# Building convolution kernels from one shared angle, in groups of four and eight channels

## The chip, the cores and the metric

The kernel runs on one core of a Trainium2 chip. The engines are named as in the profile: PE (TensorE, the matrix multiplier, with PEld for its weight loads), DVE (VectorE), ACT (ScalarE), POOL (GpSimd) and SP (SyncE, which issues DMAs). The metric is device time in microseconds (us). Each time is the median of several runs; beside it stands one profiled execution, from which all durations of single instructions come.

## The reference

Four layers follow each other, each added to x (32 x 64 x 1024, float32). The first is a long convolution per channel, the next two multiply by one of 16 matrices that an index selects, the last is a gated feed-forward layer with low-rank additions. Only the first is touched:

```python
dt = exp(log_dt)                                  # per channel h
A  = -exp(log_A_real) + 1j * A_imag               # per channel and state, 64 states
Ct = C * (exp(A * dt) - 1) / A
K  = 2 * einsum('hn,hnl->hl', Ct, exp(A * dt * arange(L))).real
y  = causal_convolution(u, K) + u * D             # L = 1024
x  = x + y * (arange(L) < length)                 # a length for each of 32 batches
```

So 64 kernels K of 1024 taps have to be made from 64 complex states each, and every channel is then convolved with its kernel. D, a number per channel, can be added to tap 0 of K.

## The kernel before

`convolution` (line 598) holds this layer; `tile_cond_resid_kernel` (line 64) calls it and goes on with the adapters (line 161) and the feed-forward layer (line 456).

**Making K.** The 128 partitions hold the 64 states twice, the upper half for imaginary parts. Position l is written as 32 a + b, so that exp(A dt l) is a product of a coarse power (a) and a fine power (b), and K as a 32 x 32 matrix is a matmul of 128 partitions: coarse powers times coefficients (`gt`) against fine powers (`et`). Small tiles (`small`, 128 x 64) hold what exists per state and channel: the step, the exponents x and y, the coefficients. Sines go through `sine` (line 638): the angle is divided by 2 pi, rounded by adding and subtracting a large number (`MAGIC`), 2 pi times that is subtracted in three parts, a phase is added, the result is clamped to pi, and ACT takes the sine. A cosine is a sine with another phase, and its own reduction.

`kernels(g)` (line 738) makes the kernels of eight channels. POOL multiplies x and y by the 32 positions (`brho`, `bth`; lines 757, 758), ACT takes Exp of the one, DVE and ACT take three sines of the other (coarse cosine, coarse sine and one fine sine; lines 641 to 649), DVE forms `bgt` and `bet` with five products and sums (lines 777 to 781), PE multiplies (line 785, eight matmuls into `pk`), ACT copies `pk` to `ks` (line 793), POOL adds D to tap 0 (line 795), and ACT issues two stores to `kp` in HBM: 128 zeros per row, which are written early, and the row itself (line 798).

**Convolving.** `convolve` (line 803) handles four channels. SP loads `uf`, x with each block of 128 positions reversed (line 806), and `hk`: for each pair of channels a 128 x 1024 matrix with overlapping windows of the stored row (line 811), three buffers. PE multiplies, eight matmuls a channel with 256, 224, ... 32 columns (line 823); DVE multiplies the result by the mask into `tmp` (line 830), and POOL adds it into the four tiles of x (line 839), which SP loaded first of all (line 622).

**Order.** PE's order is the program's own. On DVE, ACT, POOL and SP a scheduler places the instructions, from the program and a model of their times; each engine then executes strictly in that order, and waits at an instruction whose inputs or buffers aren't free. Tiles of pool `s1` have one buffer, those of `s2` two. The loop at line 842 calls `kernels` for group 0, then after the first and the second four channels, and then after each group of eight, so that PE makes a group's rows one to two groups ahead of their use. SP also issues the adapters' first weight tiles (`early`, nine of them, and then `wa`, nine buffers; line 177) where the scheduler puts them among the `hk` loads.

Of the kernel before, what the change touches and what calls it, by code (L numbers as in the profile page):

```python
# [8 lines left out]
F32 = mybir.dt.float32  # L9
I32 = mybir.dt.int32  # L10
AF = mybir.ActivationFunctionType
ALU = mybir.AluOpType
# [23 lines left out]
NE = 16  # L36
NPIECE = 2 * BC
AT_GATED, AT_DOWN = 4, 5
HG = 8
LQ = 32  # L40
KROW = P + L

# [8 lines left out]


CO_LVAL = 0
CO_PHI = CO_LVAL + 2 * LQ
CO_SGN = CO_PHI + 4
CO_POS = CO_SGN + 1
CO_R = CO_POS + KT
CO_OFF = CO_R + 1
# [539 lines left out]
def convolution(tc, cst, consts, xt, xf, ssm, lens, xs, ps_tile):  # L598
# [9 lines left out]
    with ExitStack() as ctx:  # L608
# [25 lines left out]
        def tt(o, a, b, op):  # L634
            nc.vector.tensor_tensor(o, a, b, op)
            return o

        def sine(theta, phi, turns, new):

            k, r = new("k"), new("r")  # L640
            nc.vector.tensor_scalar(k, theta, 1.0 / TWO_PI, turns, ALU.mult, ALU.add)
            nc.vector.tensor_scalar(k, k, MAGIC, MAGIC, ALU.add, ALU.subtract)
            nc.vector.scalar_tensor_tensor(r, k, -C1, theta, ALU.mult, ALU.add)
            nc.vector.scalar_tensor_tensor(r, k, -C2, r, ALU.mult, ALU.add)
            nc.vector.scalar_tensor_tensor(r, k, -C3, r, ALU.mult, ALU.add)
            nc.vector.tensor_scalar(r, r, phi, PI_IN, ALU.add, ALU.min)
            nc.vector.tensor_scalar(r, r, -PI_IN, None, ALU.max)
            s = new("s")
            nc.scalar.activation(s, r, AF.Sin)
            return s  # L650

        def exponential(v):

# [21 lines left out]
            )  # L675
            return k


        x, y = small(), small()
        ex = exponential(par[:, 0:2, :].rearrange("p i h -> p (i h)"))  # L680
        dt, ea = ex[:, :H], ex[:, H:]
        nc.vector.scalar_tensor_tensor(x, ea, -1.0, dt, ALU.mult, ALU.mult)
        tt(y, aim, dt, ALU.mult)

        t, em, ep = small(), small(), small()
        nc.scalar.activation(t, x, AF.Tanh, scale=0.5)
# [4 lines left out]

        yh = small()
        nc.vector.tensor_scalar(yh, y, 0.5, None, ALU.mult)
        sh = sine(yh, 0.0, 0.0, lambda _: small())
        ch = sine(yh, math.pi / 2, 0.25, lambda _: small())
        zr, zi, u = small(), small(), small()
        nc.vector.scalar_tensor_tensor(u, ep, 2.0, sh, ALU.mult, ALU.mult)
        tt(zi, u, ch, ALU.mult)
        tt(u, u, sh, ALU.mult)
# [7 lines left out]
        tt(v, zi, cre, ALU.mult)  # L707
        tt(ni, ni, v, ALU.add)

        den, w, ctr, cti = small(), small(), small(), small()  # L710
        tt(den, ea, ea, ALU.mult)
        tt(w, aim, aim, ALU.mult)
        tt(den, den, w, ALU.add)
        nc.vector.reciprocal(den, den)
        nc.vector.tensor_scalar(den, den, col(CO_SGN), None, ALU.mult)
        tt(ctr, ni, aim, ALU.mult)
        tt(w, nr, ea, ALU.mult)
        tt(ctr, ctr, w, ALU.subtract)
        tt(ctr, ctr, den, ALU.mult)
        tt(cti, ni, ea, ALU.mult)  # L720
        tt(w, nr, aim, ALU.mult)
        nc.vector.scalar_tensor_tensor(cti, cti, -1.0, w, ALU.mult, ALU.subtract)
        tt(cti, cti, den, ALU.mult)


        lnf = s1.tile([P, B], F32, tag="lnf", name="lnf")
        nc.vector.tensor_copy(lnf, ln)
        mask = s1.tile([P, KT, B], F32, tag="mask", name="mask")
        for kt in range(KT):
            nc.vector.tensor_scalar(  # L730
                mask[:, kt, :], lnf, col(CO_POS + kt), None, ALU.is_gt
            )
        maskf = mask.rearrange("p k b -> p (k b)")

        zero = s1.tile([HG, P], F32, tag="zero", name="zero")
        nc.vector.memset(zero, 0.0)

        def kernels(g):

            h0 = g * HG  # L740
            shape = [P, HG, LQ]

            def over_l(ap):
                return ap[:, h0 : h0 + HG].unsqueeze(2).to_broadcast(shape)

            def over_h(at):
                return cst[:, at : at + LQ].unsqueeze(1).to_broadcast(shape)

            n = [0]

            def big(tag, pool=s1):
                n[0] += 1
                return pool.tile(shape, F32, tag=f"b{tag}", name=f"b{tag}{g}_{n[0]}")

            def powers(at, tag):
                theta, rho = big(f"th{tag}"), big(f"rho{tag}")
                nc.gpsimd.tensor_tensor(theta, over_l(y), over_h(at), ALU.mult)
                nc.gpsimd.tensor_tensor(rho, over_l(x), over_h(at), ALU.mult)
                nc.scalar.activation(rho, rho, AF.Exp)
                return theta, rho  # L760

            th1, rho1 = powers(CO_LVAL, "1")
            th2, rho2 = powers(CO_LVAL + LQ, "2")

            def flat_sine(theta, i, tag):
                return sine(
                    theta.rearrange("p h l -> p (h l)"),
                    col(CO_PHI + i),
                    col(CO_PHI + 2 + i),
                    lambda q: big(q if q == "k" else f"{q}{tag}").rearrange("p h l -> p (h l)"),  # L770
                ).rearrange("p (h l) -> p h l", l=LQ)

            p1 = flat_sine(th1, 0, "p")
            q1 = flat_sine(th1, 1, "q")
            p2 = flat_sine(th2, 0, "e")
            gt, et = big("gt", s2), big("et", s2)
            tt(et, p2, rho2, ALU.mult)
            tt(p1, p1, over_l(ctr), ALU.mult)
            tt(q1, q1, over_l(cti), ALU.mult)
            tt(p1, p1, q1, ALU.add)  # L780
            tt(gt, p1, rho1, ALU.mult)

            ps = ps_tile(f"pk{g}")
            for i in range(HG):
                nc.tensor.matmul(
                    ps[:LQ, i * LQ : (i + 1) * LQ],
                    gt[:, i, :],
                    et[:, i, :],
                    start=True,
                    stop=True,  # L790
                )
            ks = s2.tile([LQ, HG, LQ], F32, tag="ks", name=f"ks{g}")
            nc.scalar.copy(ks.rearrange("a h b -> a (h b)"), ps[:LQ, : HG * LQ])
            k0 = ks[0:1, :, 0]
            nc.gpsimd.tensor_tensor(k0, k0, dskip[0:1, h0 : h0 + HG], ALU.add)
            kp = dram.tile([HG, KROW], F32, tag=f"kp{g}", name=f"kp{g}")
            nc.scalar.dma_start(kp[:, :P], zero)
            nc.scalar.dma_start(kp[:, P:].rearrange("h (a b) -> a h b", b=LQ), ks)
            return kp

        loads = []
# [1 line left out]
        def convolve(kp, row, ha):  # L803

            uf = s3.tile([P, 4, KT, B], F32, tag="uf", name=f"uf{ha}", bufs=2)
            nc.sync.dma_start(uf, xf[:, ha : ha + 4])
            tmp = s2.tile([P, 4, KT * B], F32, tag="tmp", name=f"tmp{ha}")
            for i in range(0, 4, 2):
                hk = s3.tile([P, 2, L], F32, tag="hk", name=f"hk{ha + i}")

                load = nc.sync.dma_start(
                    hk,
                    bass.AP(
                        tensor=kp.tensor,
                        offset=kp[row + i : row + i + 1, 1:2].offset,
                        ap=[[1, P], [KROW, 2], [1, L]],
                    ),
                )
                loads.append(load.ins)
                ps = ps_tile(f"pc{ha + i}").rearrange("p (i t) -> p i t", i=2)  # L820
                for j in range(2):
                    for d in range(KT):
                        nc.tensor.matmul(  # L823
                            ps[:, j, d * B :],
                            hk[:, j, d * P : (d + 1) * P],
                            uf[:, i + j, : KT - d, :].rearrange("p k b -> p (k b)"),
                            start=(d == 0),
                            stop=(d == KT - 1),
                        )
                tt(  # L830
                    tmp[:, i : i + 2, :],
                    ps,
                    maskf.unsqueeze(1).to_broadcast([P, 2, KT * B]),
                    ALU.mult,
                )
            tv = tmp.rearrange("p i (k b) -> p k b i", b=B)
            for c in range(NCK):
                xv = xs[c].rearrange("p k (b h) -> p k b h", h=H)[:, :, :, ha : ha + 4]
                nc.gpsimd.tensor_tensor(xv, xv, tv[:, :, c * BC : (c + 1) * BC, :], ALU.add)


        ready = [kernels(0)]
        for ha in range(0, H, 4):
            convolve(ready[ha // HG], ha % HG, ha)

            if len(ready) < H // HG and (ha == 0 or ha % HG == 4):
                ready.append(kernels(len(ready)))
        return loads


# [1 line left out]
def _constants(np):  # L852
# [2 lines left out]
    c = np.zeros((P, CO_N), np.float32)  # L855
    c[:, CO_LVAL : CO_LVAL + LQ] = LQ * np.arange(LQ)
    c[:, CO_LVAL + LQ : CO_LVAL + 2 * LQ] = np.arange(LQ)
    for i, turns in enumerate((np.where(im, 0.0, 0.25), np.where(im, 0.25, 0.5))):
        c[:, CO_PHI + i] = TWO_PI * turns
        c[:, CO_PHI + 2 + i] = turns  # L860
    c[:, CO_SGN] = np.where(im, -2.0, 2.0)
    c[:, CO_POS : CO_POS + KT] = p[:, None] + P * np.arange(KT)
    c[:, CO_R] = p % R
# [137 lines left out]
```

## Time and profile before

| what | us |
|---|---|
| median of 3 runs (2413.58 to 2415.15) | 2414.2 |
| the profiled execution, its own time | 2413.82 |
| its span, first to last instruction | 2412.2 |
| PE busy in the span | 2322.5 |
| DVE, ACT, POOL busy | 1115.7, 306.7, 209.9 |
| first convolution matmul starts | 41.7 |
| first adapter matmul starts | 207.4 |

The page shows busy time per engine, then 40 slices of the span, DMA queues, the chain of work that ended last, and the costliest groups. Busy PE means that matmuls are in flight, not that it is at its peak. A timeline row gives start, duration, engine, line, tiles and count, with the idle time ahead of it and what ended that. A matmul of float32 leaves two records.

### The profile page before, as it was taken

How to read it: one execution, taken by the hardware profiler on the slowest of the kernel's cores; microseconds unless marked ns; L12 is line 12 of the kernel's file. 1: busy time of each engine (PE TensorE's matmuls, PEld its weight loads, DVE VectorE, ACT ScalarE, POOL GpSimd, SP SyncE). 2: the span in 40 equal slices, each digit the busy share in tenths (PEclk: the TensorE clock that was granted, in tenths of full speed). 3: DMA queues.
4: the chain of work that ended last, by engine and by line, in shares of the span. 5: the costliest groups of instructions: out<-in, count | busy, mean ns of one | idle time of the engine just before them, and what ended most of it. 6: DMA issues, size and time to landing. Idle time of an engine off the chain costs nothing.

```text
span 2412.2 us, 46245 instructions
## 1 busy us (share of the span) xinstructions
PE 2322.5 (96%) x19136; PEld 1834.6 (76%) x19136; DVE 1115.7 (46%) x2192; ACT 306.7 (13%) x597; POOL 209.9 (9%) x294
## 2 busy tenths in 40 slices
PE   3898888999999999999999999999999999999999
PEld 3896335777887786877787786787787787888888
DVE  8911113544354453454344543454344534655653
ACT  3200001111011101110011101110011101110110
POOL 2534001000000011000000020000000020000000
PEclk9999999999999999999999999999999999999999
DMA  6789997665665656665656646656756543223311
GB/s 242 247 289 347 408 408 286 245 231 199 229 214 208 225 158 202 231 219 201 219 210 222 235 141 218 225 203 211 242 192 244 201 147 119 88 79 112 98 56 62
DMA packets 163092, 501.20 MB, mean 208 GB/s; under 512 B 19970, under 2 KB 54082, under 8 KB 161858
## 3 DMA queue, kind: packets, MB, share of 16 engines
q1 hardware_dynamic: 146402, 461.76, 54.6%
q0 software_dynamic: 9568, 27.80, 3.5%
q10 hardware_dynamic: 6912, 8.69, 1.0%
q8 instruction: 151, 2.47, 0.4%
q14 instruction: 59, 0.48, 0.1%
HBM read 485.30 MB, written 12.88 MB: 207 GB/s over the span
## 4 chain that ended last, share of the span: by engine, by line
PE 88%; DMA 9%; DVE 2%; SPq 0%; issue 0%; ACT 0%; POOL 0%; DVEq 0%; ACTq 0%
PE pf L359 40%; PE po L556 20%; PE pa L182 14%; DMA wa<-in_w 7%; PE pc L823 5%; PE pr L419 3%; PE po L551 2%; PE pe L303 2%; PE pl_d L275 1%; DMA hk<-kp 1%; DMA wl<-in_wd_rest 1%; DMA early<-in_w 0%; PE pl_u L275 0%; PE pl_g L275 0%; DMA ln<-in_lens 0%
## 5 line engine op out<-in xcount | busy, mean ns | idle before, releaser
L359 PE MATMUL pf<-xd,wf 128*128 128x256 f32 x2560 | 607.2, 381 | 0.0
L359 PEld LDWEIGHTS pf<-xd,wf 128*128 128x128 f32 x2560 | 481.6, 190 | 75.4 <-issue 7.4
L182 PE MATMUL pa<-wa,x 128*32 128x256 f32 x8048 | 469.2, 382 | 30.6 <-DMA wa<-in_w 29.3
L359 PE MATMUL pf<-xd,s 128*128 128x256 f32 x1920 | 453.6, 379 | 0.4 <-ACT c L375 0.4
L182 PEld LDWEIGHTS pa<-wa,x 128*32 128x32 f32 x8048 | 246.2, 110 | 246.2 <-DMA wa<-in_w 71.8
L359 PEld LDWEIGHTS pf<-xd,s 128*128 128x128 f32 x1920 | 364.7, 190 | 50.4 <-ACT c L375 0.8
L823 PE MATMUL pc<-uf,hk 128*128 128x256 f32 (+7 forms) x1024 | 153.5, 313 | 17.9 <-DMA hk<-kp 17.2
L823 PEld LDWEIGHTS pc<-uf,hk 128*128 128x128 f32 x1024 | 148.7, 196 | 22.3 <-DMA hk<-kp 9.7
L219 POOL DMA_INDIRECT bgu<-in_bgu,rows x44 | 46.3, 1053 | 1351.0 <-PE pe L303 1304.0
L556 PE MATMUL po<-act,wd 128*128 128x256 f32 x640 | 161.7, 383 | 0.0
L556 PE MATMUL po<-actd,wd 128*128 128x256 f32 x640 | 159.0, 379 | 0.0
L556 PE MATMUL po<-actd,s 128*128 128x256 f32 x640 | 159.0, 379 | 0.0
L384 DVE TENSOR_TENSOR c<-pf,u 128x256 f32<-128x256 f32 x80 | 33.9, 424 | 242.3 <-PE pf L359 242.3
L556 PEld LDWEIGHTS po<-act,wd 128*128 128x128 f32 x640 | 119.5, 190 | 22.9 <-issue 6.1
L556 PEld LDWEIGHTS po<-actd,s 128*128 128x128 f32 x640 | 121.6, 190 | 16.5
L556 PEld LDWEIGHTS po<-actd,wd 128*128 128x128 f32 x640 | 121.6, 190 | 16.5
L313 ACT COPY lt<-pe 128x512 f32<-128x512 f32 x160 | 82.1, 600 | 307.5 <-PE pe L303 216.1
L193 DVE STREAM_TRANSPOSE y<-pa 128x512 f32<-128x512 f32 x64 | 45.4, 710 | 145.0 <-PE pa L182 145.0
L388 DVE TENSOR_TENSOR c<-c,lt 128x1024 f32<-128x1024 f32 x80 | 97.9, 1224 | 6.7 <-DVE c L386 0.5
L331 DVE TENSOR_TENSOR s<-wf 128x512 f32<-128x512 f32 x80 | 54.6, 683 | 81.3 <-DMA wf<-in_wg 38.5
L331 DVE TENSOR_TENSOR s<-wd 128x384 f32<-128x384 f32 x64 | 31.1, 486 | 128.9 <-PE po L556 96.0
L419 PE MATMUL pr<-x,wr 128*128 128x512 f32 x192 | 84.2, 595 | 0.0
(173 smaller groups left out, 1845.0 us busy)
## 6 DMA issues: line engine op xcount, KB each, us to landing
wa<-in_w SPq DMA_DIRECT2D x503, 512.0 KB, 8.2
wf<-in_wg SPq DMA_DIRECT2D x80, 512.0 KB, 4.4
wf<-in_wu SPq DMA_DIRECT2D x80, 512.0 KB, 3.6
wd<-in_wd SPq DMA_DIRECT2D x96, 384.0 KB, 4.3
hk<-kp SPq DMA_DIRECT2D x32, 1024.0 KB, 8.1
x<-in_xt SPq DMA_DIRECT2D x4, 2048.0 KB, 10.7
uf<-in_xf SPq DMA_DIRECT2D x16, 512.0 KB, 4.4
wd<-in_wd SPq DMA_DIRECT2D x32, 256.0 KB, 3.9
```

The lines of the kernel that those rows point to most:

```text
L182: nc.tensor.matmul(acc[i * S : (i + 1) * S, s * 256 : (s + 1) * 256], xs[c][:, kt, lo + s * S : lo + (s + 1) * S], wt[:, i * 256 : (i + 1) ...
L193: nc.vector.transpose(y, acc)
L219: nc.gpsimd.indirect_dma_start(out=t, out_offset=None, in_=table, in_offset=bass.IndirectOffsetOnAxis(ap=at_, axis=0),)
L303: nc.tensor.matmul(ps[:, at_ * 2 * H : (at_ + 1) * 2 * H], bt[pair(j), g], tms[table][pair(j)], start=(g == 0), stop=True, skip_group_chec ...
L313: nc.scalar.copy(lt[:, :n, 2 * H * j : 2 * H * (j + 1)], ps[:, : n * 2 * H].rearrange("p (i t) -> p i t", i=n),)
L331: nc.vector.tensor_add(s1, a21, a22)
L359: nc.tensor.matmul(ps, ws[j][:, kt, :], xb[j][:, kt, :], start=start and kt == 0, stop=kt == KH - 1, skip_group_check=True,)
L388: nc.vector.tensor_add(cf, cf, lt[:, g].rearrange("p i t -> p (i t)"))
L419: nc.tensor.matmul(ps, wt[:, kt, :], xs[c][:, kt, :], start=(kt == 0), stop=(kt == KT - 1),)
L551: nc.tensor.matmul(pss[j], w, a, start=False, stop=False, skip_group_check=True)
L556: nc.tensor.matmul(pss[j], ws[j][:, i, :], ab[m - m0][j], start=(m == m0 and home[j] % 2 == 0), stop=(m == m1 - 1), skip_group_check=True,)
L823: nc.tensor.matmul(ps[:, j, d * B :], hk[:, j, d * P : (d + 1) * P], uf[:, i + j, : KT - d, :].rearrange("p k b -> p (k b)"), start=(d == ...
```

## The change

The coarse and the fine angle stand in one tile `r` (two times n x 32 columns) and are reduced together, without a phase (`reduced`). ACT takes the sine of the coarse angle, and gets cosines as the sine of pi/2 minus the magnitude (`cosine`), in place of a second reduction; of the fine angle, the lower 64 partitions take the cosine and the upper 64 the sine. The upper half's coefficients are written out with operands that differ by half (`ax`, `ay`). Groups are 4, 4, 8, 8, ... channels instead of 8; the Exp factors of the first two are made first, ahead of the small tiles' Tanh and Sin (`sizes`, with an ordering edge). D reaches tap 0 through a matmul: a tile `dk`, zero but for D in one column per channel, times a selecting matrix, into the same PSUM accumulation (POOL writes D into `dk`, which has one buffer). The masks are one DVE operation in place of eight, after group 1's last product, and POOL converts the lengths. The first four channels' `hk` are loaded one channel at a time. Two groups are made ahead of the first `convolve`, and group g + 2 after the first four channels of group g.

```diff
-HG = 8
+GROUPS = (4, 4, 8, 8, 8, 8, 8, 8, 8)
+HG = max(GROUPS)
...
+        def reduced(theta, k):
+            nc.vector.tensor_scalar(k, theta, 1.0 / TWO_PI, MAGIC, ALU.mult, ALU.add)
+            nc.vector.tensor_scalar(k, k, MAGIC, None, ALU.subtract)
+            for part in (C1, C2, C3):
+                nc.vector.scalar_tensor_tensor(theta, k, -part, theta, ALU.mult, ALU.add)
+            nc.vector.tensor_scalar(theta, theta, PI_IN, -PI_IN, ALU.min, ALU.max)
+            return theta
+
+        def cosine(o, r, k):
+            nc.scalar.activation(k, r, AF.Abs)
+            nc.scalar.activation(o, k, AF.Sin, scale=-1.0, bias=col(CO_HALF))
...
+        def powers(g, v, pool, tag):
+            o = big(g, tag, pool, True)
+            for i in range(2):
+                at_ = cst[:, CO_LVAL + i * LQ : CO_LVAL + (i + 1) * LQ]
+                at_ = at_.unsqueeze(1).to_broadcast([P, GROUPS[g], LQ])
+                nc.gpsimd.tensor_tensor(o[:, i], over_l(g, v), at_, ALU.mult)
+            return o
...
+        def sizes(g):
+            rho = powers(g, x, s2, "rho")
+            done = nc.scalar.activation(rho, rho, AF.Exp)
+            sized.append(done.ins)
+            return rho
...
         tt(y, aim, dt, ALU.mult)
+        rhos = {g: sizes(g) for g in range(2)}
...
-        sh = sine(yh, 0.0, 0.0, lambda _: small())
-        ch = sine(yh, math.pi / 2, 0.25, lambda _: small())
+        reduced(yh, u)
+        with tc.issue_after(sized[-1]):
+            nc.scalar.activation(sh, yh, AF.Sin)
+            cosine(ch, yh, zr)
...
+        nc.scalar.copy(ax[re], aim[re])
+        nc.scalar.mul(ax[im], ea[im], -1.0)
+        nc.scalar.copy(ay[re], ea[re])
+        nc.scalar.copy(ay[im], aim[im])
...
-        nc.vector.tensor_copy(lnf, ln)
-        for kt in range(KT):
-            nc.vector.tensor_scalar(
-                mask[:, kt, :], lnf, col(CO_POS + kt), None, ALU.is_gt
-            )
...
+        dk = s1.tile([P, HG, LQ], F32, tag="dk", name="dk")
+        nc.gpsimd.memset(dk, 0.0)
 
         def kernels(g):
-            th1, rho1 = powers(CO_LVAL, "1")
-            th2, rho2 = powers(CO_LVAL + LQ, "2")
-            p1 = flat_sine(th1, 0, "p")
-            q1 = flat_sine(th1, 1, "q")
-            p2 = flat_sine(th2, 0, "e")
+            h0, n = sum(GROUPS[:g]), GROUPS[g]
+            rho = rhos.pop(g) if g in rhos else sizes(g)
+            r = powers(g, y, s1, "r")
+            nc.gpsimd.tensor_copy(dk[0:1, :n, 0], dskip[0:1, h0 : h0 + n])
+            k, co = big(g, "k", s1, True), big(g, "co", s1, True)
+            reduced(r, k)
+            cosine(co, r, k)
+            si = big(g, "si", s1, False)
+            nc.scalar.activation(si, r[:, 0], AF.Sin)
+            nc.scalar.activation(co[im, 1], r[im, 1], AF.Sin)
...
+            ps = ps_tile(f"pk{g}")[:LQ, : n * LQ]
+            nc.tensor.matmul(
+                ps,
+                cst[:, CO_SEL : CO_SEL + LQ],
+                dk[:, :n].rearrange("p h l -> p (h l)"),
+                start=True, stop=False, skip_group_check=True,
+            )
...
-            k0 = ks[0:1, :, 0]
-            nc.gpsimd.tensor_tensor(k0, k0, dskip[0:1, h0 : h0 + HG], ALU.add)
...
+                for j in range(0, 2, 1 if ha == 0 else 2):
+                    n = 1 if ha == 0 else 2
+                    load = nc.sync.dma_start(hk[:, j : j + n], ...)
...
-        ready = [kernels(0)]
+        ready = [kernels(0), kernels(1)]
+        nc.gpsimd.tensor_copy(lnf, ln)
+        with tc.issue_after(made[1]):
+            nc.vector.tensor_tensor(
+                mask,
+                lnf.unsqueeze(1).to_broadcast([P, KT, B]),
+                cst[:, CO_POS : CO_POS + KT].unsqueeze(2).to_broadcast([P, KT, B]),
+                ALU.is_gt,
+            )
+        for g, n in enumerate(GROUPS):
+            h0 = sum(GROUPS[:g])
+            for i in range(0, n, 4):
+                convolve(ready[g], i, h0 + i)
+                if i == 0 and g + 2 < len(GROUPS):
+                    ready.append(kernels(g + 2))
```

## The prediction

> **What bounds the kernel now.** I read, in this order: the page's shares and slices, PE's timeline over the first 225 us, the chain of waits for 50 to 72 and 190 to 262 us, 2-us stretches with clock and DMA share, and the groups by form. The change touches the convolution alone, which PE leaves at 207.4 us of a span of 2412.2. PE's timeline (start, us, engine, line, tiles, [idle before <-releaser]):
>
> ```profile
> 31.10 1.06 PE L785 MATMUL pk<-bet,bgt 128*32 128x32 f32 x16 [31.10 <-DVE bet L635]
> 41.69 11.36 PE L823 MATMUL pc<-uf,hk 128*128 128x256 f32 x64 [9.53 <-DMA hk<-kp]
> 52.98 0.69 PE L785 MATMUL pk<-bet,bgt 128*32 128x32 f32 x16
> 53.60 9.38 PE L823 MATMUL pc<-uf,hk 128*128 128x256 f32 x64
> 62.92 0.69 PE L785 MATMUL pk<-bet,bgt 128*32 128x32 f32 x16
> 70.93 21.27 PE L823 MATMUL pc<-uf,hk 128*128 128x256 f32 x128 [7.32 <-DMA hk<-kp]
> ...
> 170.50 36.98 PE L823 MATMUL pc<-uf,hk 128*128 128x256 f32 x256
> 207.41 0.64 PE L182 MATMUL pa<-early,x 128*32 128x256 f32 x8
> ```
>
> PE starts at 41.69, convolves channels 0 to 7, stands 7.32 us for channel 8's `hk`, and then hardly stands again (0.3 us at 121.6, 0.7 at 132.2). Four channels take 9.38 us. So the end of the stage hangs on the moment when channel 8 starts. The chain of waits (start, us, what) says who was late:
>
> ```profile
> 57.40 0.60 DVE tmp L635
> 58.00 0.07 issue
> 58.07 4.57 POOL x L839 x4
> 62.64 0.23 POOL ks L795
> 62.89 1.54 DMA kp<-ks
> 64.45 6.35 DMA hk<-kp
> ```
>
> Kernel rows that ACT had copied at 57.5 waited in POOL's queue, behind four additions into x, for an addition of 0.23 us; ahead of that the chain is DVE's sine reductions. After the convolution the chain is one stream of weights, whose start hangs on SP's last `hk` issue (193.7, when PE frees a buffer), not on PE's work; from 373 us on it is PE:
>
> ```profile
> 249.59 10.11 DMA wa<-in_w
> ...
> 259.81 10.11 DMA wa<-in_w
> ```
>
> Eight tiles take 10.11 us, 1.26 each. What the convolution wins thus reaches the end of the kernel, as does each `early` tile loaded before that last issue. Two stretches set bounds (span, PE, PEld, DVE, ACT, POOL busy, clock, DMA share, GB/s): x is still landing until about 27 us, and after its wait PE runs at half clock:
>
> ```profile
> 24.00:26.00 2.00, 0.00 (x0) 0.00 (x0) 2.00 (x7) 1.10 (x1) 1.03 (x1) 1.00 0.92 381
> 26.00:28.00 2.00, 0.00 (x0) 0.00 (x0) 1.93 (x6) 0.69 (x2) 1.26 (x2) 1.00 0.63 250
> 72.00:74.00 2.00, 2.00 (x8) 1.93 (x7) 2.00 (x3) 0.00 (x0) 2.00 (x3) 0.50 1.01 408
> ```
>
> **What the Trainium skill says.** *VectorE: DVE Perf Modes*, "The perf-mode tier table": fp32 `tensor_scalar` between SBUF tiles runs at twice the rate of `tensor_tensor`. The trace agrees: 0.28 us against 0.42 for 256 elements, and 0.69 for 512 with two inputs; from 0.18, 0.22, 0.28 for 64, 128, 256 I estimate 0.42 for one input at 512. *GPSIMD Engine Reference*, "Specifications": SBUF interfaces are shared with VectorE. It agrees: DVE operations of 0.42 take about 1.05 while POOL adds into x at 72 us. *ScalarE: Activation LUTs*, "Table sets: the hidden batching unit": `abs` is filler in every set, so it needs no load of its own; no run here shows it yet, but loads take the 1283 ns of its section "What ACT_TABLE_LOAD costs". *TensorE: Matmul & The Clock Gate*, Part 1: after an idle window of about 3.4 us PE runs at half clock until warm. It agrees: four channels after the first wait took 11.36 instead of 9.38, eight after the second 21.27 instead of 18.7.
>
> **The change, part by part.**
>
> *Masks later.* DVE now stands from 5.1 to 8.08 for `lens` (6.24 us to land), as mask operations stand among the exponential's steps. Without them eight dependent steps of 0.33 (0.28 plus 0.05) end at 7.7 instead of 10.9; x is ready at 8.0. POOL now converts `lens` ahead of its first product, and ACT's ninth store of zeros waits for the same DMA semaphore ahead of the Tanh, so both start at about 8.5: of 3.2 us some 2.7 are won.
>
> *Groups 0 and 1.* POOL makes the x products of both groups and then group 0's y: six of 128 elements. From 0.24 us for 8 elements and 0.61 to 0.66 for 256 I take 0.45: 8.5 + 2.7 = 11.2. DVE finishes the half angle and reduces group 0's two angles in one go (two `tensor_scalar`, three two-input steps, one clamp on 256 elements: 3 x 0.28 + 3 x 0.42 + gaps = 2.4) from 12.3 to 14.7. ACT needs 0.42 + 0.31 + 0.42 + 0.31 for magnitude, sine, cosine and the imaginary half: 16.1. DVE then has 17 coefficient operations and five products, mixed with group 1's reduction, about 0.18 apart: 20.4, against 31.0 now. PE's rows: 21. ACT copies them behind group 1's first activations and stores behind its cosine: issue at about 21.9, landed 23.9.
>
> *`hk` by single channels.* Issued at 23.9, but SP's queue still holds x until about 27. Half a MB after that, with the 6.35 of the chain less 1.7: 29.7. PE starts there instead of at 41.69. The two extra issues cost 0.4 us each on SP, under x's tail; `uf` of channels 4 to 7, now behind these loads on SP, is needed only 11 us later.
>
> *The round.* Groups 2 and later run in a ring, since the angle, its multiple and the cosine have one buffer each: POOL's products 2 x 0.71, DVE's reduction of 512 (3 x 0.42 + 3 x 0.69 + gaps and POOL's share of SBUF = 3.9), ACT's magnitude 0.63, load 1.28, sine 0.42, cosine 0.63 and half sine 0.42 (3.5 with gaps). Sum 8.8. The widths of 512 are estimates from
>
> ```profile
> L635 DVE TENSOR_TENSOR tmp<-pc,mask 128x512 f32<-128x512 f32 x32 | 22.0, 689 | 77.0 <-PE pc L823 73.0 <-issue 4.0
> L649 ACT ACT_TABLE_LOAD x8 | 10.3, 1283 | 2.1 <-DVE brp L647 1.2 <-DVE brq L647 0.8
> L649 ACT ACTIVATE bsq<-brq 128x256 f32<-128x256 f32 x8 | 3.3, 417 | 19.4 <-DVE brq L647 19.4
> ```
>
> with 0.83 ns per element on ACT, from that same section (64 and 256 elements here: 0.26 and 0.42, the same slope). In the built program ACT's copy of group 2 (channels 8 to 15) stands behind the cosine of group 4, so three rounds lie ahead of it. They begin at 23.5, when DVE has made group 1's products (3 us after group 0's) and comes to the masks: 23.5 + 3 x 8.8 = 49.9 for its store, landed 51.4, `hk` landed 6.35 later: 57.7. PE comes there at 29.7 + 11.4 + 1.1 + 9.4 + 1.1 = 52.7, so it stands 5.0 us, and starts cold again as now. Now: 70.93. Won: 13.2.
>
> *D by TensorE.* The addition leaves POOL, and with it the 4.57 us above. In its place each group has a matmul 128x256; L359's take 607.2 us for 2560 records, two a matmul: 0.47. Five stand after channel 8 on the stage's bound: 2.3 lost. The earlier ones hide under the waits for `hk`. POOL's copy of D waits for PE to free `dk`, and the next products are queued behind it; PE does that matmul first after a block, when the mask product is ready too, so it delays little.
>
> *After channel 8* a round of 8.8, or 13 with x's additions, stays under PE's 18.7 + 1.1 per group; the wait of 0.7 for `bet` goes: 0.7 won. SP's order now holds four, not two, `early` tiles ahead of the last `hk`: 2 x 1.26 = 2.5 won in the stream; in the convolution, where DMA is 80 to 90% busy, I charge 0.3 for them. Everything after stands in the same order and shifts.
>
> Sum: 13.2 - 2.3 + 0.7 + 2.5 - 0.3 = 13.8. The profiled execution took 2413.82 around its span of 2412.2; 2398.4 of span, and from the median of 2414.2, 2400.4. Its own range is 2396 to 2404: half a microsecond per round, one for the first store, one for the stream.
>
> **Rivals.** *No second wait*: if rounds take under 7.1, `hk` of channel 8 lands before 52.7 and PE stays warm. Won: 70.93 - 52.7 + 2.6 for the warm clock - 2.3 + 0.7 + 2.5 - 0.3 = 21.4: 2392.8. For it: nothing in a round but sums; against it: POOL and DVE get in each other's way. *Late rounds*: 11 us each, as DVE at 0.83 to 1.05 per operation would give; channel 8 at 64.3: 2407. At 13.2 a round all is given back, 2413 to 2416. *An engine ring becomes the bound* (slower): if rounds exceed PE's 19.8 per group for good, seven of them from 23.5 on set channel 56, which PE now starts at about 188.8; less 8 for store and load that is 22.5 per round. At 24 the kernel takes 2422.5 (10.5 late, less the 2.2 of the tiles). DVE's load per group falls from 26 operations to 11 wide ones, which speaks against it. *The matmul is dear*: under half clock throughout it costs 2.3 more, 2402.7, inside the range.
>
> **How the numbers follow.** Likeliest 0.60; no second wait 0.17; late rounds 0.14; given back 0.05; slower 0.04. The range from 2392 to 2407 leaves out about 0.2. A measurement of this kernel can hardly tell 0.2% (4.8 us) from no change: faster 0.92, same 0.05, slower 0.03.
>
> **What would show it.** PE's first `pk` near 21, first `pc` near 30; a wait of about 5 us for `hk` near 53, with half clock behind it; rounds of 8.8 between POOL's y products; no wait for `bet`; the last `pc` ending near 196; wa at 10.11 per eight. Wrong it would be if ACT loads a table for the magnitude, if the first `hk` lands after 35, or if the stream loses the two tiles by waiting for PE's buffers (wa's tenth tile waits 3.9 us for PE now, with some four tiles still queued).

## The result, and the profile after

The changed kernel takes 2401.06 us (median of 4 runs, 2398.29 to 2402.67) against 2414.68 for the kernel before in the same session: a ratio of 0.9942, 95% interval 0.993 to 0.9955. The prediction was 2400.4. Its profiled execution took 2400.47 around a span of 2398.8, against 2413.82 and 2412.2.

PE's timeline of the changed kernel (start, us, engine, line, tiles, [idle before <-releaser]; `pk` takes a group's rows, `pc` the convolution of the channels):

```profile
21.01 0.63 PE L804 MATMUL pk<-bet,bgt 128*32 128x32 f32 x8 [16.56 <-DVE bgt L791]
33.44 10.90 PE L845 MATMUL pc<-uf,hk 128*128 128x256 f32 x64 [8.44 <-DMA hk<-kp]
44.27 0.62 PE L795 MATMUL pk<-dk,cst 128*32 128x256 f32 x2
44.73 0.67 PE L804 MATMUL pk<-bet,bgt 128*32 128x32 f32 x16
45.32 9.38 PE L845 MATMUL pc<-uf,hk 128*128 128x256 f32 x64
...
59.13 11.01 PE L845 MATMUL pc<-uf,hk 128*128 128x256 f32 x64 [3.37 <-DMA hk<-kp]
...
149.40 46.19 PE L845 MATMUL pc<-uf,hk 128*128 128x256 f32 x320
195.51 0.64 PE L184 MATMUL pa<-early,x 128*32 128x256 f32 x8
```

The second wait for `hk`, channel 8's, is still there, 3.37 us instead of 7.32, and channel 8 starts at 59.13 instead of 70.93: 11.8 earlier. From there to the first adapter matmul nearly the same time passes, 136.38 us against 136.48. So the stage ends 11.9 earlier (195.51, was 207.41). The first start, 8.25 earlier at 33.44, is not what counts here, since PE stands again.

The chain of waits of the changed kernel ahead of channel 8 (start, us, what):

```profile
44.61 0.99 DVE br L645
...
46.83 0.70 DVE br L645
...
50.38 0.61 ACT bco L652
50.99 0.26 ACT ks L813
...
51.27 1.57 DMA kp<-ks
...
52.86 6.13 DMA hk<-kp
...
59.13 11.01 PE pc L845 x64
```

POOL's addition and the 4.57 us in its queue are gone from it. In their place stands a round of the ring: ACT copies the rows of group 2, which PE had ready at 45.3, only at 51.0, behind the cosine of group 4. POOL's timeline shows when the rounds begin:

```profile
22.90 1.27 POOL L698 TENSOR_TENSOR br<-sm,cst 128x256 f32<-128x256 f32 x2 [0.48 <-POOL dk L778]
...
32.38 1.55 POOL L698 TENSOR_TENSOR br<-sm,cst 128x256 f32<-128x256 f32 x2 [6.50 <-DVE bco L637]
...
41.89 1.56 POOL L698 TENSOR_TENSOR br<-sm,cst 128x256 f32<-128x256 f32 x2 [5.32 <-DVE bco L637]
```

A round is 9.48 and 9.51 us from start to start, where 8.8 was predicted.

Behind the convolution the weight stream keeps what it won up to about 390 us: PE is 14.8 us ahead of the kernel before in the matmuls into `pr`. From the fourth block of those into `pf` it is 13.6 ahead, and 13.4 at the end. The 1.26 between are a balance of two waits of PE: it stands 1.50 us instead of 2.13 for the gathered `bgu`, and 2.32 instead of 0.43 for ACT's `c`. The second is seen in PE's and DVE's timelines. Before:

```profile
402.43 0.69 DVE L505 TENSOR_TENSOR wl<-wl 128x512 f32<-128x512 f32 x1 [20.62 <-DMA wl<-in_wd_rest]
...
412.67 1.99 PE L359 MATMUL pf<-xd,s 128*128 128x256 f32 x8 [0.43 <-ACT c L375]
```

and after:

```profile
388.84 0.69 DVE L507 TENSOR_TENSOR wl<-wl 128x512 f32<-128x512 f32 x1 [21.87 <-DMA wa<-in_w]
...
399.09 1.99 PE L361 MATMUL pf<-xd,s 128*128 128x256 f32 x8 [2.32 <-ACT c L377]
```

This subtraction on the weights `wl` starts 13.5 us after SP asked for the second half of them before (388.94), and 14.7 us after (374.10). Operations that feed PE's next block are queued behind it on DVE. In the changed kernel the profile puts the end of the wait down to a load of `wa`, which the subtraction doesn't read, and doesn't tell when `wl` landed; in two other versions (D alone, groups of eight) it names `wl`, 14.3 and 14.7 us after the request.

### The profile page after: what moved, and what is told of

Its sections match the earlier page's. It is cut to its first block, busy times and chain, and to the rows that moved or that the text cites. A ratio compares the mean times of both kernels' runs of the same rounds, so it can differ in the third digit from the quotient of the medians.

```text
span 2398.8 us, 46172 instructions
## 1 busy us (share of the span) xinstructions
PE 2324.7 (97%) x19154; PEld 1837.2 (77%) x19154; DVE 1087.4 (45%) x2067; ACT 310.8 (13%) x605; POOL 206.8 (9%) x301
## 4 chain that ended last, share of the span: by engine, by line
PE 90%; DMA 7%; DVE 1%; ACT 1%; issue 0%; POOL 0%; SPq 0%; ACTq 0%; DVEq 0%; POOLq 0%
PE pf L361 41%; PE po L558 20%; PE pa L184 15%; DMA wa<-in_w 6%; PE pc L845 5%; PE pr L421 3%; PE po L553 2%; PE pe L305 2%; PE pl_d L277 1%; PE pl_u L277 0%; PE pl_g L277 0%; DVE br L645 0%; DMA ln<-in_lens 0%; DMA hk<-kp 0%; DMA kp<-ks 0%
## 5 line engine op out<-in xcount | busy, mean ns | idle before, releaser
L845 PE MATMUL pc<-uf,hk 128*128 128x256 f32 (+7 forms) x1024 | 151.8, 311 | 11.8 <-DMA hk<-kp 11.8
L558 PEld LDWEIGHTS po<-actd,wd 128*128 128x128 f32 x640 | 121.6, 190 | 16.5
L558 PEld LDWEIGHTS po<-actd,s 128*128 128x128 f32 x640 | 121.6, 190 | 16.5
```

The lines of the kernel that those rows point to most:

```text
L558: nc.tensor.matmul(pss[j], ws[j][:, i, :], ab[m - m0][j], start=(m == m0 and home[j] % 2 == 0), stop=(m == m1 - 1), skip_group_check=True,)
L845: nc.tensor.matmul(ps[:, j, d * B :], hk[:, j, d * P : (d + 1) * P], uf[:, i + j, : KT - d, :].rearrange("p k b -> p (k b)"), start=(d == ...
```

## The experiments

The theory: the end of the convolution hangs on the landing of channel 8's `hk`, and that on ACT's order and three rounds of the ring; behind it come the weight tiles loaded early. The rivals: the rounds themselves, x's loads, or the stream behind the convolution bind, and the start of PE counts. Most experiments are read in the moment of the first adapter matmul (the stage's end), which a profile gives to a tenth, while the times of one version spread by 2 to 8 us over its runs. In the table "first `pc`" is the first convolution matmul and "channel 8" the moment when PE starts on that channel; a slow restart is a stretch at half clock after a wait. The kernel before gave 2414.6 to 2415.2 beside them; ratios are to it.

| version | first `pc` | channel 8 | stage's end | median, us | ratio (95%) |
|---|---|---|---|---|---|
| before | 41.69 | 70.93 | 207.41 | 2414.68 | |
| after | 33.44 | 59.13 | 195.51 | 2401.06 | 0.9942 (0.993 to 0.9955) |
| store first | 33.18 | 55.37 | 190.24 | 2396.78 | 0.9924 (0.9907 to 0.9941) |
| no D | 32.91 | 57.47 | 192.41 | 2400.21 | 0.994 (0.9924 to 0.9957) |
| before, D by TensorE | 39.46 | 64.97 | 199.96 | 2407.45 | 0.9972 (0.9961 to 0.9983) |
| groups 4, 8, ..., 4 | 33.23 | 55.45 | 190.21 | 2395.23 | 0.9919 (0.9903 to 0.9936) |
| groups of 8 | 34.44 | no wait | 191.57 | 2398.15 | 0.9932 (0.9915 to 0.9948) |
| masks early | 33.53 | 60.58 | 198.44 | 2403.22 | 0.9953 (0.9936 to 0.9969) |
| `hk` in pairs | 35.22 | 59.74 | 194.47 | 2401.5 | 0.9949 (0.9932 to 0.9965) |
| store first, x's last tile late | 28.49 | 56.27 | 192.85 | 2399.69 | 0.9936 (0.9919 to 0.9952) |
| tiles held | 32.95 | 59.12 | 196.36 | 2406.51 | 0.9962 (0.9949 to 0.9974) |
| `wl` later | 32.91 | 58.93 | 195.65 | 2398.57 | 0.9931 (0.9915 to 0.9948) |
| three edits together | 30.10 | 53.59 | 187.85 | 2391.03 | 0.9904 (0.9887 to 0.992) |

**Group 2's store ahead of group 4's activations.**

```diff
-            cosine(co, r, k)
...
-            nc.scalar.activation(si, r[:, 0], AF.Sin)
+            with ExitStack() as order:
+                if g >= 4:
+                    order.enter_context(tc.issue_after(stored[g - 2]))
+                cosine(co, r, k)
+                nc.scalar.activation(si, r[:, 0], AF.Sin)
...
+            stored.append(store.ins)
```

> The changed kernel, but from group 4 on ACT's activations of a group are ordered behind the store of the group two before it, so that group 2's rows (channels 8 to 15) no longer wait for group 4's cosine. Theory (channel 8's `hk` is late because its store stands behind three rounds in ACT's order): the store goes out near 46, right behind PE's rows of 45.4, `hk` of channel 8 lands near 53.5, before PE gets there at 55.8; no wait there and no cold restart, so 3.4 + 1.6 = 5.0 us less: first adapter matmul near 190.5 instead of 195.5, time near 2396. Rival (the rounds of POOL, DVE and ACT are late whatever the order of the store): PE waits elsewhere, for `bet` of group 4 or a later `hk`, and the stage ends at 194 to 196, time 2400 to 2401.

Measured: the stage ends at 190.24, 5.27 earlier; PE's timeline of this version has no wait in these rows and no slow restart (9.38 for four channels, not 11.01):

```profile
45.00 9.39 PE L849 MATMUL pc<-uf,hk 128*128 128x256 f32 x64
54.32 0.62 PE L798 MATMUL pk<-dk,cst 128*32 128x256 f32 x2
54.77 0.67 PE L807 MATMUL pk<-bet,bgt 128*32 128x32 f32 x16
55.37 9.38 PE L849 MATMUL pc<-uf,hk 128*128 128x256 f32 x64
```

The median is 2396.78. POOL's `br` products start at 22.97, 32.46 and 41.95, so the rounds are as long as before (9.49). They had been early enough all along; only the place of the copy in ACT's order, behind group 4's activations, made channel 8 wait.

**Groups of 4, 8, ..., 8, 4**, so that channel 8 belongs to a group made ahead of the first convolution.

```diff
-GROUPS = (4, 4, 8, 8, 8, 8, 8, 8, 8)
+GROUPS = (4, 8, 8, 8, 8, 8, 8, 8, 4)
```

> The changed kernel with groups of 4, 8, 8, 8, 8, 8, 8, 8 and 4 channels, so that channels 8 to 11 belong to group 1, whose rows are made ahead of the first convolution. Theory: PE starts at about 33.4 as now (bound by `kp`'s store behind x's loads, not by the making), and has no second wait, since group 2 is wanted only 28 us later: stage ends 5.0 earlier, near 190.5, time near 2396. Rival (making eight channels in group 1 delays group 0 or the rounds by more than the 3 to 8 us of slack that they have): first `pc` after 35, or a wait for channel 12.

Measured: first `pc` at 33.23, no wait behind it for channel 12 or for 100 us after, stage's end 190.21, 2395.23 us. Two different edits that take away the same wait give the same end to 0.03 us.

**Groups of eight only.**

```diff
-GROUPS = (4, 4, 8, 8, 8, 8, 8, 8, 8)
+GROUPS = (8, 8, 8, 8, 8, 8, 8, 8)
```

> The changed kernel with eight groups of eight channels, two of them made ahead of the first convolution, as the whole change but without groups of four. Theory: group 0's rows come near 24 instead of 21, which x's loads hide; group 1's rows, which stand ahead of the first convolution in PE's order, come near 32; PE starts near 34 and doesn't stand again, since channel 16 is wanted 40 us later: stage ends near 191.8 instead of 195.5. Three `early` tiles instead of four: 1.3 given back in the stream; time near 2398.6. Rival (groups of four are what makes the start early): start after 37, stage at 195 or later, time 2401 or more.

Measured: start at 34.44, stage's end 191.57, 2398.15 us. The small groups make the first rows 1.9 earlier (21.01 against 22.91) but start PE only 1.0 earlier, since in both kernels the first store lands behind x's loads (SP could ask for `hk` at 29.32 and 30.35), and they bring the second wait: in this kernel two groups of four cost 3.9 us of stage.

The versions in which PE does not stand for channel 8 have something in common that the changed kernel hides. From the first `pc` to the stage's end they take 157.06 (store first), 156.98 (groups 4, 8, ..., 4) and 157.13 us (groups of eight). So once the second wait is gone, it is the start that sets the end.

**`hk` in pairs.**

```diff
-                for j in range(0, 2, 1 if ha == 0 else 2):
-                    n = 1 if ha == 0 else 2
+                for j in range(0, 2, 2):
+                    n = 2
```

> The changed kernel with the first four channels' `hk` loaded in pairs as before. Theory: first `pc` about 1.4 us later (half a MB more ahead of it), near 34.8, but channel 8's `hk` lands when it did, so PE stands 2.0 instead of 3.4 us for it: stage ends at 195.5, time 2401, or 1.6 less where the shorter idle time leaves PE's clock up. Rival (what PE starts later it ends later): stage at 196.9, time 2402.5.

Measured: first `pc` 1.8 later, at 35.22, and the stage's end 1.0 earlier, at 194.47, because PE now waits 2.29 for channel 8 and doesn't slow down. The time, 2401.5, can't be told from the changed kernel's. A later start that costs nothing at the end shows again that the start is not on the path while PE stands for channel 8.

**Masks early.**

```diff
+        nc.vector.tensor_copy(lnf, ln)
+        for kt in range(KT):
+            nc.vector.tensor_scalar(mask[:, kt, :], lnf, col(CO_POS + kt), None, ALU.is_gt)
...
-        nc.gpsimd.tensor_copy(lnf, ln)
-        with tc.issue_after(made[1]):
-            nc.vector.tensor_tensor(mask, ..., ALU.is_gt)
```

> The changed kernel with the masks as before: DVE converts the lengths and makes eight masks among the exponential's steps. Theory: DVE stands for `lens` until 8.1 us, x is ready at about 10.9 instead of 7.9, POOL's first product starts at 11.1 instead of 8.55, and rounds and store of group 2 are 2.6 later: first `pk` rows near 23.6, first `pc` unchanged near 33.4 (its store lies behind x's loads until 29), `hk` of channel 8 near 61.6, stage ends near 198.1, time near 2403.7. Rival (the start of the convolution is bound by x's loads, so what is won ahead of them is worth nothing): stage at 195.5, time 2401.

Measured: rows at 22.65, first `pc` at 33.53, channel 8 at 60.58, stage's end 198.44, 2403.22 us. The end is where it was expected, the way there is not. POOL's first product starts at 11.42, 2.9 later (2.6 was expected), but the rows are only 1.6 later and channel 8 only 1.45. The other 1.5 of the stage's 2.9 arise behind channel 8: 0.74 in a slower restart (11.75 for four channels) and 0.59 in a wait for `hk` at 180 us. What swallows the early lead in the changed kernel stands in its DVE timeline:

```profile
8.67 2.13 DVE L719 TENSOR_SCALAR sm<-sm 128x64 f32<-128x64 f32 x1 [0.25 <-ACT sm L718]
```

An operation of 64 elements, 0.20 just before, takes 2.13; it ends with POOL's six products, which run from 8.55 to 10.74. And the half angle's sine comes 1.65 earlier than in this version (13.24 against 14.89), not 2.9. That POOL held it up is inferred from the times; in the version with early masks the same operation took 0.38 beside the same products.

**D by TensorE, alone, in the kernel before.**

```diff
+            nc.gpsimd.tensor_copy(dk[0:1, :, 0], dskip[0:1, h0 : h0 + HG])
...
+            nc.tensor.matmul(ps[:LQ, : HG * LQ], cst[:, CO_SEL : CO_SEL + LQ],
+                             dk.rearrange("p h l -> p (h l)"), start=True, stop=False, ...)
...
-            k0 = ks[0:1, :, 0]
-            nc.gpsimd.tensor_tensor(k0, k0, dskip[0:1, h0 : h0 + HG], ALU.add)
```

> The kernel before with one part of the change, D by TensorE instead of POOL's addition; groups of eight, sines and masks as before. Theory (4.57 us behind POOL's additions into x and 0.23 for its own): channel 8's `hk` lands 4.8 earlier, near 66.0; PE is there at 64.1, stands 2 us instead of 7.3 and so keeps its clock, which saves another 2.6; five matmuls of 0.44 cost 2.2; stage ends 5.2 earlier, near 202.2, or 2.6 earlier if PE restarts cold. Four `early` tiles instead of two: 2.5. Time 7.7 less, 2407.0 (5.1 less without the warm clock). Rival (POOL's wait was not the cause of the stall): stage at 207.4 plus the matmuls, 209.6, and time 2414.4.

Measured: channel 8 at 64.97, stage's end 199.96, 2407.45 us (8 runs, 2403.86 to 2410.53). PE's timeline of this version:

```profile
61.25 0.67 PE L798 MATMUL pk<-bet,bgt 128*32 128x32 f32 x16
64.97 18.56 PE L835 MATMUL pc<-uf,hk 128*128 128x256 f32 x128 [3.04 <-DMA hk<-kp]
```

Eight channels take 18.56 and not 21.27: no slow restart. The stage's end is 2.2 better than expected: channel 8 starts 1.0 before the 66.0 that was said, and 1.2 less passes behind it, 0.8 of that because the waits of 0.3 and 0.7 in the kernel before shrink to one of 0.2. PE's first rows came at 29.78 instead of 31.10; that was not followed further. So D alone, which takes the store out from behind POOL's additions, brings about half of the whole change's 13.6 us (7.2 by the medians, 0.28% against 0.58% by the ratios). That includes two more weight tiles ahead of the last `hk`, for which 2.5 had been estimated.

**No D at all**, so that D is missing from the result.

```diff
-            nc.tensor.matmul(ps, cst[:, CO_SEL : CO_SEL + LQ], dk..., start=True, stop=False, ...)
...
-                    start=False,
+                    start=True,
```

> The changed kernel without the matmul of D (it leaves D out of the result). Theory (five of these matmuls lie on the stage's bound, 0.44 each; two weight tiles ahead of the last `hk` are worth 1.26 each in the stream): first adapter matmul 2.2 earlier, near 193.3. In its built order only two `early` tiles stand ahead of the last `hk`, so the stream gives 2.5 back: time the same to 0.5, near 2401. Rival (the tiles are worth nothing, they are loaded somewhere anyway): 2.2 less at the end too, 2398.9. Rival (the D matmul hides behind something): first adapter matmul unchanged at 195.5.

Measured: stage's end 192.41, 3.1 earlier. Of that, 1.66 is channel 8's earlier start (in this order ACT copies the rows one activation earlier, at 49.3 instead of 51.0), and the rest the five matmuls, 5 x 0.43 = 2.15, less 0.7 that is lost later on, 0.55 of it in a wait for `hk` at 173 us. The time, 2400.21, is the changed kernel's: of the 3.1 the stream, with two tiles fewer ahead of it, had given back 2.3 by 360 us.

**All tiles held behind the last `hk`.**

```diff
-    with tc.issue_after(blocks[5]):
+    with tc.issue_after(blocks[-1]):
```

> The changed kernel with the adapters' first weight tiles held back until after the last `hk` load: none of the nine `early` tiles stands ahead of it instead of four; the other engines' order is as it was. Theory (each tile ahead of the last `hk` shortens the stream behind it by the 1.26 us that one takes): first adapter matmul unchanged near 195.5 or up to 0.5 earlier, since the loads leave the convolution's stretch; the stream ends 4 x 1.26 = 5.0 later, time near 2406. Rival (the tiles only fill a queue that PE's buffers hold up anyway): no more than 1 us later, 2401 to 2402.

Measured: 2406.51 us, 5.5 more, or 4.8 by the ratios, for four tiles. Of that 0.85 arose in the stage: channel 8 starts at 59.12 as in the changed kernel, but the restart behind it was slower (11.72 instead of 11.01), and the stage ends at 196.36. It did not come earlier, so the early tiles cost the convolution nothing that can be seen.

**DVE's subtraction on `wl` behind `rest`.**

```diff
-        rest(c)
+        made_rest = rest(c)
...
-                nc.vector.tensor_sub(wl[:, 1, 0], wl[:, 1, 0], wl[:, 1, 1])
+                with tc.issue_after(made_rest):
+                    nc.vector.tensor_sub(wl[:, 1, 0], wl[:, 1, 0], wl[:, 1, 1])
```

> The changed kernel, but DVE's subtraction on the half-gathered weights `wl`, which the last block alone uses, is ordered behind the last product of `rest` (one ordering edge; nothing of the convolution is touched). Theory: of the 14.8 us that the weight stream had won by 389 us, 1.26 are lost where this subtraction waits for `wl` (landed 14.7 after its issue instead of 13.5) with nine DVE operations queued behind it, and PE then waits 2.3 for ACT's `c`. Without that: no such wait, the stage's end unchanged at 195.5, and 2.3 less at the end, near 2398.8. Rival (PE waits there for `bgu` or the weights `wf` in any case, and DVE's wait only covers that): time unchanged, 2401.

Measured: 2398.57 us. The stream of this run stood 0.7 behind the changed kernel's at 360 us and 2.2 ahead of it at 411, and PE no longer waits for `c`, so the place is confirmed: it cost more than the 1.26 given back, since the kernel before had paid there too. Why the subtraction started 14.7 instead of 13.5 us after the request stays open; in the other versions with the old order it was 14.3 to 15.0.

**x's last tile behind the first loads of `hk`**, on top of the first edit.

```diff
-        for c in range(NCK):
+        for c in range(3):
             nc.sync.dma_start(xs[c], xt[:, c])
...
+                if ha == 4 and i == 2:
+                    with tc.issue_after(loads[-1]):
+                        for c in range(3, NCK):
+                            nc.sync.dma_start(xs[c], xt[:, c])
+                    add(late.pop(), 0)
```

> The version with group g's activations behind the store of group g - 2 (e1), and the last of x's four tiles is loaded behind the first four channels' `hk` and the next two pairs, with block 0's additions into x after that. Theory (the first store took 7 us because x's 8 MB lay ahead of it on the DMA engines): it lands near 24 instead of 29, first `pc` starts near 28.4 instead of 33.2, no wait for a later `hk`; stage ends near 185.5 instead of 190.2, time near 2392. Rival (the engines have no room for x's last tile later either, or POOL, waiting for it, holds up the rounds): a wait for `hk` or `bet` after the start gives back 2 to 5 us, stage at 188 to 190.5.

Measured: first `pc` at 28.49, as expected, but a wait of 5.08 for channel 8 and the stage's end at 192.85. The chain of waits of this version, ahead of channel 8:

```profile
42.03 0.37 ACT ks L816
...
42.42 7.42 DMA kp<-ks
...
49.86 6.28 DMA hk<-kp
...
56.27 3.76 PE pc L862 x12
```

The copy is early. But the store, which takes 1.57 in the changed kernel, takes 7.42 here, behind x's tile and `hk`, which SP had issued at 35.6 and before. The expectation failed by its own mechanism: what the first store was spared, group 2's met. The rival named x's tile as the trouble, not this store.

**Three edits together**: groups 4, 8, ..., 8, 4, `wl` later, and x's last tile late, where the next store wanted is issued ahead of that load.

> Three of the edits together: groups of 4, 8, ..., 8, 4 (e4), DVE's subtraction on `wl` behind `rest` (e6), and x's last tile loaded behind the first six loads of `hk`, with block 0's additions after that (as in e11, where it collided with group 2's store; here the store that is wanted next is group 1's, issued near 29, ahead of that load). Theory: group 0's store, issued at 24.4, lands near 26 instead of 29.1; first `pc` near 30.0 instead of 33.2; no wait for a later `hk`, as group 2 is wanted only 28 us later; stage ends near 187.0, and with the 2.2 of `wl` the time is near 2389.8. Rival (stores and `hk` of channel 4 collide with the loads again): a wait for `hk` gives back 2 to 4, time 2392 to 2394.

Measured: 2391.03 us, 0.9904 of the kernel before (0.9887 to 0.992), the fastest version here. The chain of waits of this version at the first start, and at its end ahead of channel 8:

```profile
24.66 1.43 DMA kp<-ks
...
26.11 3.95 DMA hk<-kp
...
30.10 11.06 PE pc L860 x64
...
41.63 11.83 DMA hk<-kp
```

The store takes 1.43. A wait of 1.02 for channel 8 remains: its `hk` takes 11.83, behind the loads that were put off. That is why the stage ends at 187.85 and not at 187.0. Against the groups of 4, 8, ..., 4 alone the start is 3.1 and the end 2.4 earlier: with the second wait almost gone, the earlier start counts.

## Why the prediction was right, and where it was not

- **Masks later: right for x, too large behind it.** x was used from 8.4 on (8.5 predicted), and the rows came at 21.01 (21 predicted). But undone, the step moves the rows by 1.6 and channel 8 by 1.45, where 2.7 was said: DVE's part beside POOL's products was taken at its usual rate, and one operation there took 2.13.
- **The first store: wrong, at no cost.** The step said issue at 21.9, landing at 23.9. It was issued at 22.04, and SP could ask for the first `hk` only at 29.32. The prediction counted x's loads in SP's queue but not against ACT's store, so the first `pc` came at 33.44 and not at 29.7. (The 29.7 doesn't follow from its own terms either: 6.35 less 1.7, so 4.65, after 27 would be 31.7, and after 23.9 it would be 28.6.) PE then reached channel 8 at 55.8 instead of 52.7 and simply waited less. The version with x's tile put off started at 28.49: the missing term was x's loads.
- **The round: right in kind, 0.7 too small.** POOL took 1.55 (1.42 predicted), DVE 4.36 (3.9), ACT 3.4 (3.5). DVE is the larger part: its reduction steps take 0.99 while POOL makes the next exponents and 0.70 otherwise, as the chain shows, and other operations stand between them. `hk` of channel 8 landed at 59.0 instead of 57.7, and channel 8 won 11.8 instead of 13.2.
- **The slow restart: taken over from before, and smaller.** Half clock after channel 8 cost 2.6 before and 1.63 after (11.01 less 9.38). This 1.0 and the two later waits of 0.7 and 0.3, all gone, make up for the D matmuls (136.38 us behind channel 8, was 136.48).
- **D's matmul: right.** 0.43 each (from a block's end to the next block PE takes 1.05 with it, 0.62 without), five of them 2.2; 2.3 was said. No table load came with the magnitude.
- **Early tiles: right in size.** Behind the stage the stream won a further 2.9 by 360 us (2.5 predicted for two tiles); four tiles held back cost 4.8 to 5.5, or 4.0 to 4.6 without the 0.85 of the stage. No charge in the convolution was found.
- **"Everything after stands in the same order and shifts": wrong by 1.26.** The wait of DVE's subtraction on `wl`, and of PE for what is queued behind it, was not in any step.

The sum was 13.8 of span and 13.4 was measured; 1.4 too much at channel 8 and 1.26 at `wl` stand against 1.0 at the restart, 0.3 for a charge not incurred, 0.3 for the wait at 121.6 us, which no step had counted, 0.4 more in the stream, and some 0.3 in small pieces. The mechanism held: channel 8's wait remained, behind three rounds and ACT's order. But steps that were off by 1.0 to 1.4 us each way cancelled, so part of the closeness is luck.

Of the rivals, "no second wait" rested on rounds under 7.1 us, and they took 9.5; but its outcome can be had without faster rounds: with ACT's order changed the wait is gone. That version ends at 2396.8 and not at 2392.8, mostly because PE gets to channel 8 2.7 us later than that rival had it, and because of `wl`. The shared angle, for itself, was not run; groups of eight with all the rest of the change end 8.4 earlier than the kernel before with D alone, and that includes the shares of the masks, of the order and of the single `hk` loads.

## What to carry to other kernels

Ask for which data the busiest engine stands last: as long as PE stood for channel 8, its start could move without moving the end in step, and a group boundary or one place in an engine's order decided. With that wait gone, the start decided, so look again after each step. When a transfer is moved out of one small store's way, look up which store comes next. An instruction that is needed late but placed early in an in-order queue makes everything behind it wait for its data.

## What the runs showed of the hardware

A store of 32 KB from ACT's queue landed after 1.57 us with the DMA engines idle (changed kernel, group 2, a DMA share of 0.00 to 0.03 ahead of it), and after 7.42 us behind loads on SP's queue (x's tile late). One of 16 KB landed after 1.43 us with the share at 0.19 (three edits together), and after 6.86 behind x's loads (store first). The Trainium skill, *DMA: Bandwidth & Descriptors*, "Queues, rings and completion order", says that each DMA engine takes turns between queues, packet by packet; by that a small store should slip in between. It did not here, and the trace's count of packets shows that the packets themselves were late: of the store issued at 42.42 with x's tile late none had moved by 45.0, while SP's queue kept the engines 95 to 107% busy. By 46.0 it was 4 of 272, and 133 and 103 followed in the next two microseconds, as SP's share fell to 83% and 29%. The changed kernel's first store, issued at 22.04, has none before 25.0 either. The measurement decides; what held the packets back stays open.

A DVE operation can take far longer beside POOL than by the factor of 2.5 that the prediction had read off the kernel before: the one of 2.13 us shown above is ten times its usual 0.20, and ends with POOL's six products. It took 0.38 beside the same products in another run, so this is not the rule.

The length of PE's idle time did not alone decide the slow restart (half clock): 2.29 (pairs) and 3.04 us (D alone) left four channels at 9.4, while after 2.46 (no D) they took

```profile
57.47 11.02 PE L836 MATMUL pc<-uf,hk 128*128 128x256 f32 x64 [2.46 <-DMA hk<-kp]
```

as after 3.37. *TensorE: Matmul & The Clock Gate*, Part 1, has a window of about 3.4 us that runs freely, so that the place of the idle time counts beside its length; that 2.46 were enough is not covered by it.
